# Attention with a threshold search: the test for points in reach only in the last search update, and other places for the work beside a turn

## The chip, the cores and the metric

The kernel runs on one core of one Trainium2 chip. The metric is the device time in microseconds of one execution. Times before the change: 4861.07, 4864.83 and 4874.88 us, median 4864.83. One further execution was taken with the hardware profiler on; the profile and the trace are of that one.

## The reference, cut to what matters

The program is two layers of a network on a tensor of 4 images, 256 channels, 32 x 32 points: attention, a mixture of experts, a selective scan, and a second mixture of experts. The change touches the attention alone. For each image and each of 8 heads it forms 1024 x 1024 scores, keeps in each row the `dyn_k` largest ones (one number for all rows, from the data), takes the softmax over them, and multiplies with the values. A depthwise 3 x 3 convolution of the values is added before the projection:

```python
attn = jnp.einsum('bhdn,bhdm->bhnm', q, k) * SCALE
dyn_k = jnp.floor(N * jnp.mean(g)).astype(jnp.int32)
order = jnp.argsort(-attn, axis=-1)
ranks = jnp.argsort(order, axis=-1)
attn = jnp.where(ranks < dyn_k, attn, -jnp.inf)
attn = jax.nn.softmax(attn, axis=-1)
out = jnp.einsum('bhdn,bhmn->bhdm', v, attn).reshape(Bx, C, Hh, Ww)
pe = lax.conv_general_dilated(v_img, pe_w, ..., feature_group_count=C) + pe_b[None, :, None, None]
return conv1x1(out + pe, proj_w, proj_b)
```

## The kernel before

**Halves and turns.** The scores are cut into 64 halves, in the order image, group of four heads, pair, half: 128 query rows by 1024 keys for four heads. Instead of sorting, the kernel searches for each row the threshold that leaves `dyn_k` scores above it. A half passes through four turns of the pipeline; `turn(i)` (L716) works on half i (h0), i-1 (h1), i-2 (h2) and i-3 (h3) and on one pair of finished halves. 16 turns belong to one image. The order of all instructions is written out by hand (`manual_schedule`, L781): each engine executes its own part of the list in that order.

In a turn, in order: PE forms the second half of h0's scores (`scores(1)`, L526) and ACT copies them out of PSUM (`take`, L534, four copies); PE forms the weights of the pair (`weights`, L637, and L642, which subtracts a large number from the scores that the masks mark: the drop matmuls); DVE takes windows of h3 (L551, L554); DVE makes the first update of the search (`update`, L592, called at L735); ACT counts h0 at the guess (L500, four counts). Then **place 0**. ACT takes the exponential (`exps`, L650), PE multiplies with the values (`sums`, L660); DVE finishes h3's windows; ACT and DVE count h1 (L500, L504). **Place 1.** PE forms the pair's second weights; DVE enters h0 into the search and makes the second update (L759); ACT and DVE count h2; POOL makes the four masks of h3 (`mask`, L584), which wait for the second update by a dependency put in by hand (L585 to L589), and six small operations (`verify`, L573 to L578). **Place 2.** Exponentials, counts of h0. **Place 3.** `start(i + 1)` (L710): first `due` (L706), then the first half of the next scores. Counts of h1, the second `sums`. **Place 4.** The mask buffers are one deep for the odd half of a pair and two deep for the even one (L583).

**The update.** `update` keeps for each row a bracket of two thresholds with their counts. The point just counted replaces one end of it, and a new point is interpolated (L601 to L611). Then L613, L615 and L616 move the point only where the count was not within reach of the aim (plus or minus 7.5): points in reach stay. After the last update the point is kept (L544), counted once more, and the exact threshold is picked among seven scores next to it. If a row's point should not be in reach then, `attention_by_bits` (L787) computes the whole attention again, under an `If` on the data (L966).

**The work beside.** Each place calls `beside(i)` (L691). It takes one stretch from a list `todo` of generators, each with a turn from which it may run and a turn by which it must be done. A generator yields True where a PE stretch has just been issued (its result lies in the only bank "m" of PSUM, L262 of the printed lines' neighbourhood: `bank`), and False after the eviction of that bank; `beside` goes on until a True. So at each place the stretch before is evicted and the next one issued. The generators:

- `Group.steps`: q and k of four heads (L343; evictions L347, L350 on ACT), the transpose of k (L358, eviction L360), second moments (L364; L367 on DVE), mq (L375; L377), mo_ps (L381, L382), then the first guess of the thresholds: L386 to L390 on DVE, a square root as a power on POOL (L391), L394, and in the next step L400 to L405 on DVE. 12 stretches.
- `Image.values`: v transposed (L424, eviction L428 on ACT), 4 stretches.
- `Image.rest`: v padded (L440, L443), for each half of the channels nine diagonals on POOL (L450, one buffer) and the convolution in six stretches of three matmuls (L455, eviction L460 on ACT), then the projection (L468, eviction L472 on DVE). 20 stretches.
- `Image.finish`: the projection of the attention's output (L481, L484), 4 stretches.

Before a turn starts, `due` runs whatever has to be done by then, without a pause. In the kernel before, from turn 16b of image b: group 1 from turn +5 (by +8), values 1 from +8, the rest from +9 (by +20), the next image's group 0 from +13 (by +16), its values 0 from +16, finish from +21 (by +23).

Of the kernel before, what the change touches and what calls it, by code (L numbers as in the profile page):

```python
# [17 lines left out]
ALU = mybir.AluOpType  # L18
# [34 lines left out]
def metaformer(ctx: ExitStack, tc: tile.TileContext, t: dict, out: bass.AP):  # L53
    nc = tc.nc
# [8 lines left out]
    first = cons.tile([P, E], F32, tag="first", name="first")  # L63
# [117 lines left out]
    with ExitStack() as st:  # L181
# [39 lines left out]
        with tc.tile_pool(name="a_ln", bufs=2) as lp, \  # L221
                tc.tile_pool(name="a_lnp", bufs=4, space=PSUM) as psl:
            g1 = load(lp, "g1", [P, CT, P], t["g1"].rearrange("(c p) o -> p c o", p=P))
            for b in range(B):
# [3 lines left out]
                for h in range(NHALF):  # L228
# [9 lines left out]
                    i = b * NHALF + h  # L238
# [350 lines left out]
                                                               mybir.DependencyReason.DATA))  # L589
                    self.drops.append(dr)  # L590

        def update():  # L592

            def flat(a):
                return a.rearrange("p k n j -> p k (n j)")

            st_ = flat(state)
            br = bracket.rearrange("p e k n j -> p e k (n j)")
            t, u = st_[:, 0], st_[:, 1]
            pick = p2.tile([P, 2, R], I32, tag="pick", name="pick", bufs=1)  # L600
            nc.vector.scalar_tensor_tensor(pick, u.unsqueeze(1).to_broadcast([P, 2, R]), aim, side,  # L601
                                           ALU.is_lt, ALU.not_equal)
            nc.vector.copy_predicated(br, pick.unsqueeze(2).to_broadcast([P, 2, 2, R]),
                                      st_.unsqueeze(1).to_broadcast([P, 2, 2, R]))
            dd = p2.tile([P, 2, R], F32, tag="dd", name="dd", bufs=1)
            nc.vector.tensor_tensor(dd, br[:, 1], br[:, 0], ALU.subtract)
            nc.vector.reciprocal(dd[:, 1, :], dd[:, 1, :])
            fr = p2.tile([P, R], F32, tag="fr", name="fr", bufs=1)
            nc.vector.scalar_tensor_tensor(fr, br[:, 0, 1, :], aim, dd[:, 1, :], ALU.subtract, ALU.mult)
            nc.vector.tensor_tensor(fr, fr, dd[:, 0, :], ALU.mult)  # L610
            nc.vector.tensor_tensor(fr, br[:, 0, 0, :], fr, ALU.subtract)  # L611
            low = p2.tile([P, R], F32, tag="low", name="low", bufs=1)
            nc.vector.tensor_scalar(low, u, aim_lo, None, ALU.is_le)  # L613
            move = p2.tile([P, R], I32, tag="move", name="move", bufs=1)
            nc.vector.scalar_tensor_tensor(move, u, aim_hi, low, ALU.is_ge, ALU.add)  # L615
            return nc.vector.copy_predicated(t, move, fr)  # L616

        def to_u(lanes, first_dve):

            ud = state[:, 1, lanes, first_dve:]  # L620
            nc.vector.tensor_scalar(ud, ud, 2.0, -float(L), ALU.mult, ALU.add)
# [52 lines left out]
        groups = {(b, g): Group(b, g) for b in range(B) for g in range(2)}  # L674
        images = [Image(b) for b in range(B)]
# [1 line left out]
        PER = 2 * NT  # L677


        todo = [[0, 0, groups[0, 0].steps(), False], [0, 0, images[0].values(0), False]]  # L680
        for b in range(B):
            i = b * PER
            todo.append([i + 5, i + 8, groups[b, 1].steps(), False])
            todo.append([i + 8, i + 13, images[b].values(1), False])
            if b + 1 < B:
                todo.append([i + 13, i + 16, groups[b + 1, 0].steps(), False])
                todo.append([i + 16, i + 21, images[b + 1].values(0), False])
            todo.append([i + 9, i + 20, images[b].rest(), False])
            todo.append([i + 21, i + 23, images[b].finish(), False])

        def beside(i):  # L691

            while True:
                ready = [w for w in todo if w[0] <= i]
                if not ready:
                    return
                w = next((w for w in ready if w[3]), None) or min(ready, key=lambda w: w[1])
                try:
                    w[3] = next(w[2])
                except StopIteration:  # L700
                    todo.remove(w)
                    w[3] = False
                if w[3]:
                    return

        def due(i):  # L706
            while any(w[1] <= i for w in todo):
                beside(i)

        def start(i):  # L710
            due(i)
            halves.append(Half(i, *order[i]))
            halves[i].group = groups[halves[i].b, halves[i].g]
            halves[i].scores(0)

        def turn(i):  # L716
            def half(d):
                return halves[i - d] if 0 <= i - d < len(halves) else None

            h0, h1, h2, h3 = (half(d) for d in range(4))  # L720

            pair, q = pairs.get((i - 5) // 2 if i % 2 else (i - 6) // 2), 0 if i % 2 else 2
            done = pairs.get((i - 7) // 2) if i % 2 else None

            if h0:
                h0.scores(1)
                h0.take()
            if pair:
                pair.weights(q)
            if h3:  # L730
                h3.window(0)
                h3.window(1)
            if half(1) or half(2):
                to_u(slice(0, 2), FIRST_DVE[1])
                update()  # L735
            if h2:
                h2.keep_threshold()
            if done:
                done.norm()
            if h0:  # L740
                h0.count(4, h0.at_guess)
            beside(i)
# [9 lines left out]
            beside(i)  # L752
            if pair:
                pair.weights(q + 1)
            if h0:
                h0.enter()
            if h1:
                to_u(slice(h1.lane, h1.lane + 1), FIRST_DVE[0])
            after = update() if h0 or h1 else None  # L759
            if h2:  # L760
                h2.count(FIRST_DVE[0], h2.at_last)
            if h3:
                h3.mask(after)
                h3.verify()
                if h3.n == 1:
                    pairs[h3.i // 2] = Pair(halves[h3.i - 1 : h3.i + 1], images[h3.b])
            beside(i)
# [4 lines left out]
            beside(i)  # L772
# [6 lines left out]
            beside(i)  # L779
# [316 lines left out]
    with ExitStack() as st:  # L1096
# [207 lines left out]
        scans, steps, ys, cum = [], iter(()), [], None  # L1304
# [37 lines left out]
        with tc.manual_schedule():  # L1342
            for k in range(-2, len(order) + 1):
                turn(k)
# [5 lines left out]
    with ExitStack() as st:  # L1350
# [12 lines left out]
        with ExitStack() as sa:  # L1363
# [3 lines left out]
            def tmp(name, shape, dt=F32):  # L1367
                return pa.tile([P, *shape], dt, tag=name, name=name)
# [54 lines left out]
            steps = tmp("steps", [NTA * P // T])  # L1423
# [11 lines left out]
            place = tmp("place", [E, NTA])  # L1435
# [175 lines left out]
```

## Time and profile before

| | |
|---|---|
| median of 3 runs | 4864.83 us |
| the profiled execution | 4900.55 us |
| its span, first to last instruction | 4898.8 us |
| mean granted TensorE clock | 0.856 |
| first and last masks of the attention (L584) | 213.0 and 2061.2 us |
| masks, L584 | x256, 724.6 us busy on POOL, 2848 ns each |
| counts on ACT, L500, state | x448, 514.1 us, 1148 ns each |
| counts on DVE, L504, state | x320, 408.6 us, 1277 ns each |
| copies on ACT, L534 | x256, 246.4 us, 1014 ns each |

Of the page, part 1 gives busy time and share for each engine, and part 2 cuts the span into 40 slices of 122 us with the busy share in tenths; the attention lies in slices 2 to 17. Part 5 lists groups of equal instructions with busy time, mean and the idle time before them. A line of the timeline gives start and length in microseconds, engine, line of the kernel, operation, tiles, and in square brackets how long the engine had been idle and what released it.

### The profile page before, as it was taken

To read this page: it belongs to the slowest core of one execution; us is meant where nothing else is said; L and a number is where in the kernel's file an instruction comes from. 1 tells how busy PE (TensorE), PEld (TensorE's weight loads), DVE (VectorE), ACT (ScalarE), POOL (GpSimd) and SP (SyncE) were. 2 spreads that over 40 slices of the span, in tenths; PEclk is the share of its full clock that TensorE was granted. 3 is DMA by queue.
4 is the path that set the end of the run, shared out by engine and by line. 5 is a ranking of instruction groups with operands and counts; after the bars stand their busy time and mean duration, and the time that the engine had idled before them with its cause. 6 is when DMAs were issued, how large, how long until landed. Compare 5 with 4: busy or idle time off the path is not lost.

```text
span 4898.8 us, 51450 instructions
## 1 busy us (share of the span) xinstructions
PE 4004.6 (82%) x18714; PEld 2228.5 (45%) x18714; DVE 3255.5 (66%) x5263; ACT 2894.4 (59%) x3813; POOL 1405.0 (29%) x1126
## 2 busy tenths in 40 slices
PE   7378777877787777689999799989989994599993
PEld 4143434343434343356666333434433432488882
DVE  2687897789778887732223799999999995111212
ACT  3788898788878978522111666677666762122221
POOL 0244444545445454510000122222222223200004
PEclk8578767877797678778999899999999997799995
DMA  3000000000000000010000223323323334334433
GB/s 128 0 1 9 1 1 1 9 1 1 1 9 1 1 1 9 1 36 1 0 1 3 78 92 112 103 87 112 104 86 112 112 111 146 118 115 121 119 109 107
DMA packets 128616, 264.86 MB, mean 54 GB/s; under 512 B 29017, under 2 KB 77282, under 8 KB 127586
## 3 DMA queue, kind: packets, MB, share of 16 engines
q1 hardware_dynamic: 118144, 243.15, 15.3%
q0 software_dynamic: 6144, 16.79, 1.1%
q8 instruction: 150, 2.46, 0.2%
q10 hardware_dynamic: 4066, 1.55, 0.1%
q14 instruction: 112, 0.92, 0.1%
HBM read 224.74 MB, written 36.70 MB: 53 GB/s over the span
## 4 chain that ended last, share of the span: by engine, by line
PE 29%; DVE 19%; issue 3%; SPq 2%; ACT 2%; DMA 1%; POOL 0%; another core or an unknown queue 0%; ACTq 0%; DVEq 0%; POOLq 0%
PE hp L1505 6%; PE yp L1511 6%; PE y L1012 5%; PE hp L1005 5%; DVE h L1284 4%; DVE h L1269 4%; DVE h L1260 4%; PE hp L1255 3%; DVE yc L1294 2%; SPq L1478 2%; DVE h L1278 1%; PE y L1295 1%; PE hp L1288 1%; ACT da_c L1242 0%; PE y L173 0%
## 5 line engine op out<-in xcount | busy, mean ns | idle before, releaser
L584 POOL TENSOR_SCALAR dr<-s_n,last 128x1024 bf16<-128x1024 f32 x256 | 724.6, 2848 | 955.2 <-DVE state L616 598.7
L1240 POOL TENSOR_TENSOR uu<-dx,bb 128x1024 f32<-128x1024 f32 x128 | 317.4, 2480 | 1521.3 <-issue 807.9
L500 ACT ACTIVATE junk_a<-s_n,state 128x1024 int8<-128x1024 f32 x448 | 514.1, 1148 | 21.7 <-DVE state L616 11.7
L1255 PE MATMUL hp<-h,ident 128*128 128x512 f32 x1024 | 496.9, 608 | 27.3 <-DVE h L1278 19.0
L1242 ACT ACTIVATE da_c<-delta,a_log 128x1024 f32<-128x1024 f32 x128 | 270.0, 2109 | 307.1 <-DVE h L1284 307.1
L504 DVE TENSOR_SCALAR_CACHE_REDUCE junk_v<-s_n,state 128x1024 int8<-128x1024 f32 x320 | 408.6, 1277 | 8.0
L1507 ACT ACTIVATE hid<-hp,b 128x256 f32<-128x256 f32 x312 | 145.1, 473 | 415.4 <-PE hp L1505 415.4
L534 ACT COPY s_n<-sp 128x1024 f32<-128x1024 f32 x256 | 246.4, 1014 | 227.0 <-PE sp L526 166.8
L551 DVE SCALAR_TENSOR_TENSOR w<-s_n,win 128x1024 f32<-128x1024 f32 x256 | 359.3, 1403 | 5.5
L1014 DVE SCALAR_TENSOR_TENSOR acc<-y,tk_comb,acc 128x256 f32<-128x256 f32 x256 | 121.0, 484 | 356.0 <-PE y L1012 352.1
L660 PE MATMUL o_ps<-ex,vT 128*32 128x256 f32 x2048 | 274.1, 490 | 83.8 <-ACT ex L650 81.0
L1514 DVE TENSOR_TENSOR ys<-yp,b2e 128x512 f32<-128x512 f32 x39 | 27.0, 692 | 467.4 <-PE yp L1511 467.4
L1255 PEld LDWEIGHTS hp<-h,ident 128*128 128x128 f32 x1024 | 191.3, 193 | 304.3 <-issue 202.5
L554 DVE MAX8 win<-w 128x8 f32<-128x1024 f32 x256 | 314.5, 1228 | 8.8
L1255 PE MATMUL hp<-h,twice 128*128 128x512 f32 x512 | 258.8, 625 | 64.1 <-DVE h L1260 40.6
L500 ACT ACTIVATE junk_a<-s_n,guess 128x1024 int8<-128x1024 f32 x256 | 295.0, 1152 | 6.2
L1260 DVE TENSOR_TENSOR_SCAN h<-da,uu 128x1024 f32<-128x1024 f32 x128 | 290.1, 2266 | 3.6 <-ACT da L1248 3.6
L1284 DVE TENSOR_TENSOR_SCAN h<-da_c,uu 128x1024 f32<-128x1024 f32 x128 | 292.3, 2284 | 0.0
L1007 ACT ACTIVATE hid<-hp,b 128x512 f32<-128x512 f32 x128 | 88.0, 687 | 345.6 <-PE hp L1005 344.8
L1269 DVE TENSOR_TENSOR_SCAN h<-da,uu 128x1024 f32<-128x1024 f32 x128 | 289.9, 2264 | 0.0
L1505 PE MATMUL hp<-xe,w 128*128 128x256 f32 x1248 | 280.8, 383 | 7.5 <-DVE xe L1498 7.5
L650 ACT ACTIVATE ex<-sT 128x1024 f32<-128x1024 f32 x256 | 246.4, 1012 | 63.1 <-PE sT L642 62.7
(480 smaller groups left out, 8147.7 us busy)
## 6 DMA issues: line engine op xcount, KB each, us to landing
bb<-bc_d SPq DMA_DIRECT2D x128, 512.0 KB, 4.8
cb<-bc_d SPq DMA_DIRECT2D x128, 512.0 KB, 4.0
w<-in_w SPq DMA_DIRECT2D x47, 1024.0 KB, 5.0
slots_x<-zeros SPq DMA_DIRECT2D x1, 9984.0 KB, 32.4
xs<-slots_x SPq DMA_DIRECT2D x39, 256.0 KB, 3.1
slots_y<-ys SPq DMA_DIRECT2D x39, 256.0 KB, 2.4
b2e<-in_b SPq DMA_DIRECT2D x39, 128.0 KB, 3.8
x_in<-in_x SPq DMA_DIRECT2D x4, 1024.0 KB, 7.9
```

The lines of the kernel that those rows point to most:

```text
L500: nc.scalar.activation(junk, self.row(r), AF.Sign, bias=thr, scale=-1.0, accum_out=u)
L504: nc.vector.tensor_scalar(junk, self.row(r), thr, None, ALU.is_lt, ALU.add, accum_out=u)
L551: nc.vector.scalar_tensor_tensor(w, self.row(r), self.win[:, r, 0:1], self.row(r), ALU.is_gt if r < LAST_DVE else ALU.is_ge, ALU.subtract, ...
L554: nc.vector.max(out=self.win[:, r, 1:], in_=w)
L584: ins = nc.gpsimd.tensor_scalar(dr, self.row(r), self.last[:, r : r + 1], None, ALU.is_lt)
L1240: nc.gpsimd.tensor_tensor(self.uu[:, 0], self.prep.dx[:, c], self.bb, ALU.mult)
L1255: nc.tensor.matmul(self.hp[h], ident if eye is None else eye, view[:, ts(h, HW // NHALF), :], start=first, stop=False)
L1260: nc.vector.tensor_tensor_scan(rows.rearrange("p r w -> p (r w)"), self.da, self.uu[:, 0], 0.0, ALU.mult, ALU.add)
L1269: nc.vector.tensor_tensor_scan(hs[:, ::-1], self.da[:, ::-1], self.uu[:, 0][:, ::-1], 0.0, ALU.mult, ALU.add)
L1284: nc.vector.tensor_tensor_scan(hs, self.da_c, self.uu[:, 1], 0.0, ALU.mult, ALU.add)
L1505: nc.tensor.matmul(hp[:, f % 2], w1[:, c, ts(f, P)], xe[:, c], start=(c == 0), stop=(c == CT - 1))
L1511: nc.tensor.matmul(yp[:, a], hid[:, f, ts(a, P)], w2e[:, f, :], start=(f == 0), stop=(f == NF - 1))
```

## The change

`update` takes an argument. With `stay=True` (the first update of a turn, which is also the last one of a half) it is as before. With `stay=False` (the second update of a turn) the interpolated point is written to the state at once, and the three instructions of the test are left out. The list of work gets places: a turn is five places, a generator may start at a given place, and takes new stretches only in places that it is given. A stretch that was begun is carried on in any place. `rest` gets places 1 and 3, the groups places 1 to 4, and the groups may start 2 places into the turn that is one earlier than before. `due` has no place: it takes anything that is ready.

```diff
-        def update():
+        def update(stay):
...
             nc.vector.tensor_tensor(fr, fr, dd[:, 0, :], ALU.mult)
+            if not stay:
+                return nc.vector.tensor_tensor(t, br[:, 0, 0, :], fr, ALU.subtract)
             nc.vector.tensor_tensor(fr, br[:, 0, 0, :], fr, ALU.subtract)
...
+        PLACES = 5
+        todo = []
+
+        def plan(first, needed, steps, places=range(PLACES)):
+            todo.append([first, needed, steps, False, places])
+
+        plan(0, 0, groups[0, 0].steps())
+        plan(0, 0, images[0].values(0))
         for b in range(B):
             i = b * PER
-            todo.append([i + 5, i + 8, groups[b, 1].steps(), False])
-            todo.append([i + 8, i + 13, images[b].values(1), False])
+            plan((i + 4) * PLACES + 2, i + 8, groups[b, 1].steps(), (1, 2, 3, 4))
+            plan((i + 8) * PLACES, i + 13, images[b].values(1))
             if b + 1 < B:
-                todo.append([i + 13, i + 16, groups[b + 1, 0].steps(), False])
-                todo.append([i + 16, i + 21, images[b + 1].values(0), False])
-            todo.append([i + 9, i + 20, images[b].rest(), False])
-            todo.append([i + 21, i + 23, images[b].finish(), False])
-
-        def beside(i):
+                plan((i + 12) * PLACES + 2, i + 16, groups[b + 1, 0].steps(), (1, 2, 3, 4))
+                plan((i + 16) * PLACES, i + 21, images[b + 1].values(0))
+            plan((i + 9) * PLACES, i + 20, images[b].rest(), (1, 3))
+            plan((i + 21) * PLACES, i + 23, images[b].finish())
+
+        def beside(i, place=None):
 
             while True:
-                ready = [w for w in todo if w[0] <= i]
-                if not ready:
+                ready = [w for w in todo if w[0] <= i * PLACES + (place or 0) and (place is None or place in w[4])]
+                w = next((w for w in todo if w[3]), None) or min(ready, key=lambda w: w[1], default=None)
+                if w is None:
                     return
-                w = next((w for w in ready if w[3]), None) or min(ready, key=lambda w: w[1])
                 try:
                     w[3] = next(w[2])
                 except StopIteration:
...
                 to_u(slice(0, 2), FIRST_DVE[1])
-                update()
+                update(stay=True)
...
-            after = update() if h0 or h1 else None
+            after = update(stay=False) if h0 or h1 else None
```

The five calls `beside(i)` of a turn become `beside(i, 0)` to `beside(i, 4)`.

More of the change, by code (lines that the diff above doesn't have):

```diff
@@ L677, in metaformer @@
         PER = 2 * NT
-        todo = [[0, 0, groups[0, 0].steps(), False], [0, 0, images[0].values(0), False]]
+        PLACES = 5
[4 more added lines that the diff above has]
+        plan(0, 0, images[0].values(0))
         for b in range(B):
             i = b * PER
-            todo.append([i + 5, i + 8, groups[b, 1].steps(), False])
-            todo.append([i + 8, i + 13, images[b].values(1), False])
+            plan((i + 4) * PLACES + 2, i + 8, groups[b, 1].steps(), (1, 2, 3, 4))
+            plan((i + 8) * PLACES, i + 13, images[b].values(1))
             if b + 1 < B:
-                todo.append([i + 13, i + 16, groups[b + 1, 0].steps(), False])
-                todo.append([i + 16, i + 21, images[b + 1].values(0), False])
-            todo.append([i + 9, i + 20, images[b].rest(), False])
-            todo.append([i + 21, i + 23, images[b].finish(), False])
-        def beside(i):
+                plan((i + 12) * PLACES + 2, i + 16, groups[b + 1, 0].steps(), (1, 2, 3, 4))
[3 more added lines that the diff above has]
+        def beside(i, place=None):
             while True:
-                ready = [w for w in todo if w[0] <= i]
-                if not ready:
+                ready = [w for w in todo if w[0] <= i * PLACES + (place or 0) and (place is None or place in w[4])]
+                w = next((w for w in todo if w[3]), None) or min(ready, key=lambda w: w[1], default=None)
+                if w is None:
                     return
-                w = next((w for w in ready if w[3]), None) or min(ready, key=lambda w: w[1])
                 try:
@@ L741, in turn @@
                 h0.count(4, h0.at_guess)
-            beside(i)
+            beside(i, 0)
             if pair:
@@ L751, in turn @@
                 h1.count(FIRST_DVE[0], h1.at_state)
-            beside(i)
+            beside(i, 1)
             if pair:
@@ L766, in turn @@
                     pairs[h3.i // 2] = Pair(halves[h3.i - 1 : h3.i + 1], images[h3.b])
-            beside(i)
+            beside(i, 2)
             if pair:
@@ L771, in turn @@
                 h0.count(FIRST_DVE[1], h0.at_state)
-            beside(i)
+            beside(i, 3)
             if i + 1 < len(order):
@@ L778, in turn @@
                 pair.sums(q + 1)
-            beside(i)
+            beside(i, 4)
         with tc.manual_schedule():
```

## The prediction

> **What bounds the kernel now.** I read the page first, then the timeline of each engine in the stage that the diff touches, from about 150 to 2060 us. On the page of the kernel before:
>
> ```profile
> PE 4004.6 (82%) x18714; PEld 2228.5 (45%) x18714; DVE 3255.5 (66%) x5263; ACT 2894.4 (59%) x3813; POOL 1405.0 (29%) x1126
> ...
> PEclk8578767877797678778999899999999997799995
> ```
>
> The shares are averages over four stages; only the first third is attention, and there the share of the span tells little: ACT, DVE and PE are each busy 75 to 85%. So I looked for what ends last in one quiet turn (no stretch beside it), turn 18. POOL, ACT and DVE in the timeline:
>
> ```profile
> 650.14 11.30 POOL L584 TENSOR_SCALAR dr<-s_n,last 128x1024 bf16<-128x1024 f32 x4 [13.24 <-DVE state L616]
> ...
> 676.85 11.30 POOL L584 TENSOR_SCALAR dr<-s_n,last 128x1024 bf16<-128x1024 f32 x4 [13.82 <-DVE state L616]
> ```
> ```profile
> 661.47 1.93 ACT L534 COPY s_n<-sp 128x1024 f32<-128x1024 f32 x2 [1.35 <-POOL dr L584]
> ```
> ```profile
> 647.75 0.23 DVE L601 SCALAR_TENSOR_TENSOR pick<-state,aim,side 128x16 int32<-128x16 f32 x1 [1.75 <-ACT junk_a L500]
> ...
> 649.17 0.17 DVE L611 TENSOR_TENSOR fr<-bracket,fr 128x8 f32<-128x8 f32 x1
> ...
> 649.77 0.17 DVE L616 COPY_PREDICATED state<-move,fr 128x8 f32<-128x8 int32 x1
> ```
>
> This is a ring: masks on POOL (11.3 us), then ACT's last two copies wait for the last mask, four guess counts, two exps, three state counts (12.3 us from 661.47 to 673.8), then the second update on DVE (2.2 us), then 0.2 us to the next masks. One round is 26.1 us when ACT is last and 26.7 when DVE is (turn 19, where the norm of a pair adds 2.2 us to DVE). I measure turns from mask start to mask start (POOL timeline). From turn 20 to turn 36, one image, old: 20 to 24 127.6 us, 24 to 28 129.7, 28 to 31 89.0, 31 to 32 26.1, 32 to 36 105.7; sum 478.1, where 16 quiet turns would take 422. The rest, 56 us an image, is what the stretches beside the turns cost.
>
> **Part 1, the update.** 65 times three instructions (L613, L615, L616) go, and L611 writes the state itself. On the ring that is 649.94 (end of L616) less 649.34 (end of L611): 0.60 us a turn, and quiet turns become 25.5 and 26.1. It pays only where masks wait for DVE. In even turns the masks of the odd half (one buffer) also wait for PE's drop matmuls, whose first quarter ended at 649.1; so 0.4 us of slack to PE are left there. 0.6 times 65, 39 us, is the upper end, nothing the lower.
>
> **Part 2, the stretches move.** Following the new plan by hand and in the changed kernel's instruction order, the same 20 conv stretches, 12 group stretches, 4 of values and 4 of finish run in other places. Prices: a conv stretch of three matmuls took 2.84 us or 4.21 (rows below), one of two 128x512 matmuls 2.0 to 2.75, a vT one 1.9 to 2.1. PE waits 2.88 us at place 0 of a quiet turn, so that place hides a stretch; places 1 and 2 to 4 have 0.4 to 1.6 us.
>
> - Turns 24 to 28: the conv's first eight stretches were five a turn, and now are two or three. One at place 1 of an odd turn is free (its masks have a second buffer); in an even one it costs its length less 0.4. I get 26.3 + 27.8 + 26.1 + 33.0 = 113.2, 16.5 less. The 33.0: a conv stretch at place 1 of turn 27 leaves PE 3 to 4 us late, two more precede the next scores, and one at place 1 of turn 28 precedes its drops.
> - Turns 20 to 24, the group with finish. Starting it a turn earlier puts q and k stretches at places 2, 3, 4 of turn 20, each waiting for ACT's eviction of the one before, as in old turn 29, where ACT's copies ended 3.1 us late. 30.4 + 29.7 + 30.6 + 38.6 = 129.3, 1.7 more. The last is as before: guess is still forced at the end of turn 23 and waits for POOL (row 809.70 below).
> - Turns 28 to 31: conv and group mixed; mp leaves place 1 of an even turn (2 us less): 29.4 + 29.4 + 29.6 = 88.4, 0.6 less.
> - Turns 32 to 36: conv, values and proj in turns that were quiet: 28.6 + 28.2 + 27.6 + 25.6 = 110.0, 4.3 more.
> - Turn 31 to 32 is the step that decides. The group now reaches its square root (L391 on POOL) at place 3, behind the four masks of the turn, not ahead of them. The forced call then evicts the guess and goes on to the next stretch that is ready: the first conv matmuls of the second half of channels, whose nine diagonals (L450) stand behind the square root on POOL. In PE's order these three matmuls come before the next half's scores. The old trace shows both waits apart:
>
> ```profile
> 804.23 5.44 POOL L391 TENSOR_TENSOR sd<-sd,half 128x32 f32<-128x32 f32 x1
> ```
> ```profile
> 809.70 0.25 DVE L400 SCALAR_TENSOR_TENSOR guess<-sd,z,mo 128x32 f32<-128x32 f32 x1 [6.97 <-POOL sd L391]
> ```
> ```profile
> 870.92 6.95 POOL L450 TENSOR_SCALAR diag<-ident,pe_w 128x128 f32<-128x128 f32 x9
> ```
> ```profile
> 871.58 2.84 PE L455 MATMUL ap__6310<-vpad,diag 128*128 128x512 f32 x6 [1.07 <-POOL diag L450]
> ...
> 929.81 4.21 PE L455 MATMUL ap__6771<-vpad,diag 128*128 128x512 f32 x6 [1.92 <-ACT x L460]
> ```
>
> Masks and the six small POOL operations take 12.9 us (791.38 to 804.23), the square root 5.4: the first diagonal is ready 19.0 us after the masks began, the third 20.6. PE would reach this point about 5 us after it, so it idles some 14 us, with the scores behind it: scores 1.1 to 2.1, sums 1.8 to 3.4, the next conv stretch 2.8 to 4.2, half of the next scores 0.6 to 1. ACT's second copy starts at 27.5 to 32 and the copies end at 30.5 to 35, against 13.3 in a quiet turn. Plus 10.5 to the end of the state counts, and then, because a conv stretch at place 1 of even turn 32 waits for ACT's eviction (0.7), runs (2.8 to 4.2) and precedes the drops (1.5 to 2.4): 46 to 53. I take 49.5, 23.4 more. It happens three times (turns 15, 31, 47).
>
> What the Trainium skill says against the change: "TensorE: Matmul & The Clock Gate", Part 1, "What's actually happening", holds that the array's clock is throttled by default and released by sustained activity. The rows 871.58 and 929.81 (2.84 and 4.21 us for the same work) and the PEclk digits of 7 and 8 here, 9 later, agree. By that rule a thinner conv would run its stretches nearer to 4.2, and with all nine exposed stretches of an image at that end the sum would grow by about 6 us an image.
>
> **The sum.** An image in the middle: +1.7 - 16.5 - 0.6 + 23.4 + 4.3 = +12.3, twice. The first image (turns 3 to 20, 490 us): its first group is spread without a finish, -6; conv -14; -0.6; +23.4; +4.2: +7. The last: +1.7 - 14.5, and its second conv half runs on in turns 60 to 64, +9: -4. The update in the first turns: -1. Sum 7 + 24.6 - 4 - 1 = +26 us in the profiled execution (4900.55 us, its span 4898.8). That execution lies 36 us above the median of 4864.83; I carry the difference over: 4891 us.
>
> **Rivals.**
> - The guess alone (no change): if PE does not lose its 14 us, because DVE's late guess holds the turn anyway. The old turn 23 to 24, with that wait, took 39.2; less 0.6 gives 38.6 for 31 to 32, 11 less than mine, three times: 26 - 33 = -7, 4858 us. For it: the same DVE wait of 6.97 us is there. Against: ACT's copies need PE's scores, and PE's queue has the conv matmuls ahead of them.
> - Faster, the other side: the slack of PE takes up what is put at places 2 to 4, so that the update's 0.6 us is paid out in turns 20 to 24, 28 to 31 and 32 to 36 as well. Old times less 0.6 a turn: 4.1 + 1.2 + 6.7 = 12 less an image, three times, and 11 in the last: 26 - 47 = -21, 4844 us. It decides once such stretches delay ACT's second copy by less than about 1.3 us (the wait for POOL at 661.47). Against: old turn 29 lost 3.1 us in this way.
> - The count at the last update misses its window without the test before it, and the whole attention runs again by bits: 4 x 8 x 256 counts of 1.277 us (L504) are 10.5 ms more. The last update keeps the test and its bracket is only narrower; 1 in 100.
>
> **Chances.** Forecast 0.55; worse still 0.03; guess alone 0.22; faster 0.19; by bits 0.01. About 0.3%, 15 us, is what this measurement can tell from no change. Faster 0.19, same 0.22, slower 0.59. The range: three stalls of 38.6 and half of the second rival's gain give 4848, stalls of 53 and half of the conv's gain lost 4925; the gain of the update is between its ends in both.
>
> **What would show it.** Masks 25.5 and 26.1 us apart in quiet turns for part 1. In turns 15, 31, 47 a PE wait of 10 us or more for diag L450, and mask to mask of 46 or more: if it is under 40, the decisive step is wrong. Turns 24 to 28 near 113 us. If turns 20 to 24 and 32 to 36 come out below the old 127.6 and 105.7, the second rival holds.

## The result and the profile after

The changed kernel takes 4884.84 us (median of 4 runs, 4880.53 to 4887.95) against 4865.09 us before (median of 4, 4861.07 to 4874.88): a ratio of 1.0037, 95% interval 1.0019 to 1.0055. It is slower by 20 us. Run once more with the experiments, on another chip, it took 4911.9 against 4890.25 us: 1.0044 (1.0027 to 1.0061). The chips differ by 25 to 31 us for one and the same kernel before, so from here on times are compared as ratios and differences within one chip; spans inside the attention are compared over chips, and each is of a single profiled execution. The profiled executions are no total either: what follows the last masks is untouched by the change and took 2837.6 us in the profile of before (4898.8 less 2061.2), 2809.1 in the first profile of the changed kernel (4878.8 less 2069.7) and 2826.0 in the second.

The page of the changed kernel, first profile:

```profile
PE 3963.8 (81%) x18714; PEld 2195.7 (45%) x18714; DVE 3211.0 (66%) x5068; ACT 2897.6 (59%) x3813; POOL 1416.6 (29%) x1126
...
PEclk8577777777777777888999899999999997799996
```

195 DVE instructions less (65 times three), a little less of PE and DVE, the same clock of 0.856: nothing here tells that the kernel is slower. So first a turn that shows the ring alone: turn 60, in which PE has conv stretches to run, but nothing waits for them. POOL, ACT and DVE:

```profile
1920.28 11.30 POOL L584 TENSOR_SCALAR dr<-s_n,last 128x1024 bf16<-128x1024 f32 x4 [16.70 <-DVE junk_v L504]
...
1945.76 2.85 POOL L584 TENSOR_SCALAR dr<-s_n,last 128x1024 bf16<-128x1024 f32 x1 [5.57 <-DVE state L612]
```
```profile
1931.61 1.93 ACT L534 COPY s_n<-sp 128x1024 f32<-128x1024 f32 x2 [0.57 <-POOL dr L584]
```
```profile
1944.02 0.23 DVE L601 SCALAR_TENSOR_TENSOR pick<-state,aim,side 128x16 int32<-128x16 f32 x1 [1.86 <-ACT junk_a L500]
...
1945.43 0.17 DVE L612 TENSOR_TENSOR state<-bracket,fr 128x8 f32<-128x8 f32 x1
```

The ring is the same, and it is 25.48 us long, not 26.1: the second update ends with L612 at 1945.60, 1.58 us after its first instruction, where it took 2.2. Part 1 does what it says.

Now turn 31. POOL, DVE and PE:

```profile
1035.87 11.30 POOL L584 TENSOR_SCALAR dr<-s_n,last 128x1024 bf16<-128x1024 f32 x4 [13.95 <-DVE state L612]
...
1048.71 5.44 POOL L391 TENSOR_TENSOR sd<-sd,half 128x32 f32<-128x32 f32 x1
1054.14 6.04 POOL L450 TENSOR_SCALAR diag<-ident,pe_w 128x128 f32<-128x128 f32 x9
1084.81 2.85 POOL L584 TENSOR_SCALAR dr<-s_n,last 128x1024 bf16<-128x1024 f32 x1 [24.62 <-PE sT L644]
```
```profile
1054.19 0.36 DVE L400 SCALAR_TENSOR_TENSOR guess<-sd,z,mo 128x32 f32<-128x32 f32 x1 [12.60 <-POOL sd L391]
```
```profile
1054.81 4.86 PE L455 MATMUL ap__7583<-vpad,diag 128*128 128x512 f32 x6 [14.42 <-POOL diag L450]
1059.60 1.14 PE L526 MATMUL sp<-k__6858,q 16*128 16x512 f32 x8
...
1065.31 1.14 PE L526 MATMUL sp<-k__6858,q 16*128 16x512 f32 x8
...
1080.40 2.84 PE L455 MATMUL ap__7737<-vpad,diag 128*128 128x512 f32 x6 [2.32 <-ACT x L460]
```
```profile
1060.83 1.01 ACT L534 COPY s_n<-sp 128x1024 f32<-128x1024 f32 x1 [17.50 <-PE sp L526]
1066.48 2.84 ACT L534 COPY s_n<-sp 128x1024 f32<-128x1024 f32 x3 [4.64 <-PE sp L526]
```

Read it from POOL: four masks, six small operations, the square root, the diagonals, without a gap from 1035.87 to 1060.2. DVE waits 12.6 us for the square root, PE 14.4 us for the first diagonal; the scores (L526) are behind PE's wait, and ACT's copies behind the scores. The next masks come 48.94 us after the last ones, where it was 26.13. The operand of the square root was there at 1041.6 (DVE, L390), 7.1 us before POOL began it. In the kernel before, turn 31 has the square root ahead of its masks, and no diagonals behind them:

```profile
1043.83 5.46 POOL L391 TENSOR_TENSOR sd<-sd,half 128x32 f32<-128x32 f32 x1 [12.02 <-DVE sd L390]
1049.28 11.30 POOL L584 TENSOR_SCALAR dr<-s_n,last 128x1024 bf16<-128x1024 f32 x4
```

The Trainium skill says as much ("PSUM — Partial Sum Buffer", "Engine vs sequencer instructions": the queues of ScalarE, VectorE and GpSimd, here ACT, DVE and POOL, are strictly first in, first out, and matmuls start in program order).

One view adds this up over the whole execution. What ended the idle time ahead of the instructions on the tile diag (us, times), in the changed kernel, and in the kernel before:

```profile
  POOL diag L450: 85.9, 12
```
```profile
  POOL diag L450: 6.7, 12
```

All stages, in us from mask start to mask start (L584), with the numbers of the prediction. The second column of the changed kernel is its second profile:

| turns | before | predicted | changed | changed, again |
|---|---|---|---|---|
| 3 to 20 | 490.0 | 497 | 499.6 | 499.4 |
| 20 to 24 | 127.6 | 129.3 | 133.5 | 133.1 |
| 24 to 28 | 129.7 | 113.2 | 109.2 | 109.2 |
| 28 to 31 | 89.0 | 88.4 | 85.0 | 90.0 |
| 31 to 32 | 26.1 | 49.5 | 48.9 | 51.4 |
| 32 to 36 | 105.7 | 110.0 | 108.5 | 107.8 |
| 20 to 36, one image | 478.1 | 490.4 | 485.1 | 491.5 |
| 52 to 65, the last | 380.4 | 376 | 370.6 | 370.1 |
| 3 to 65 | 1826.8 | | 1839.6 | 1852.6 |

The conv spread over more turns gives 20 us an image, and the turn of the guess takes 23 to 25 of them back.

### The profile page after: what moved, and what is told of

It is laid out like the page before. It is cut to its first block, busy times and chain, and to the rows that moved or that the text cites. A ratio compares the mean times of both kernels' runs of the same rounds, so it can differ in the third digit from the quotient of the medians.

```text
span 4878.8 us, 51245 instructions
## 1 busy us (share of the span) xinstructions
PE 3963.8 (81%) x18714; PEld 2195.7 (45%) x18714; DVE 3211.0 (66%) x5068; ACT 2897.6 (59%) x3813; POOL 1416.6 (29%) x1126
## 5 line engine op out<-in xcount | busy, mean ns | idle before, releaser
L584 POOL TENSOR_SCALAR dr<-s_n,last 128x1024 bf16<-128x1024 f32 x256 | 729.8, 2868 | 995.1 <-DVE state L612 501.3
L500 ACT ACTIVATE junk_a<-s_n,state 128x1024 int8<-128x1024 f32 x448 | 514.3, 1148 | 25.9 <-DVE state L618 12.1
L1265 PE MATMUL hp<-h,ident 128*128 128x512 f32 x1024 | 499.6, 611 | 27.1 <-DVE h L1288 18.9
L662 PE MATMUL o_ps<-ex,vT 128*32 128x256 f32 x2048 | 305.3, 514 | 182.7 <-ACT ex L652 177.4
L551 DVE SCALAR_TENSOR_TENSOR w<-s_n,win 128x1024 f32<-128x1024 f32 x256 | 349.1, 1364 | 5.4
L662 PE MATMUL o_ps<-ex,ones 128*32 128x256 f32 x2048 | 290.6, 502 | 0.0
## 6 DMA issues: line engine op xcount, KB each, us to landing
slots_x<-zeros SPq DMA_DIRECT2D x1, 9984.0 KB, 31.9
```

Of the source, the lines that this page charges most:

```text
L500: nc.scalar.activation(junk, self.row(r), AF.Sign, bias=thr, scale=-1.0, accum_out=u)
L551: nc.vector.scalar_tensor_tensor(w, self.row(r), self.win[:, r, 0:1], self.row(r), ALU.is_gt if r < LAST_DVE else ALU.is_ge, ALU.subtract, ...
L584: ins = nc.gpsimd.tensor_scalar(dr, self.row(r), self.last[:, r : r + 1], None, ALU.is_lt)
L662: nc.tensor.matmul(self.o_ps[32 * j : 32 * j + 32, w], ones if w else vT[:, m, ts(j, HD)], self.ex[j // 2][:, j % 2, mm], start=(m == 0 an ...
L1265: nc.tensor.matmul(self.hp[h], ident if eye is None else eye, view[:, ts(h, HW // NHALF), :], start=first, stop=False)
```

## The experiments

Eleven more runs followed, one of them the changed kernel itself. Two theories were to be told apart first. Mine: POOL's order makes the long turn, in two steps; the square root behind the masks makes the guess late, and the diagonals behind both hold PE with the next scores behind it. The rival: the late guess alone holds the turn.

| run | against before, us (ratio, 95%) | 20 to 24 | 24 to 28 | 28 to 31 | 31 to 32 | 3 to 65 |
|---|---|---|---|---|---|---|
| update_only | -22.9 (0.9946 to 0.9973) | 128.8 | 126.7 | 91.9 | 26.2 | 1811.1 |
| places_only | +37.9 (1.0071 to 1.0098) | 137.5 | 111.0 | 87.3 | 49.6 | 1865.7 |
| due_needed | -8.9 (0.9976 to 0.9995) | 136.0 | 109.2 | 86.8 | 38.6 | 1829.5 |
| diag_act | -17.4 (0.9955 to 0.9980) | 136.5 | 109.1 | 90.0 | 39.8 | 1819.9 |
| after_again | +21.7 (1.0027 to 1.0061) | 133.1 | 109.2 | 90.0 | 51.4 | 1852.6 |
| group_all | -38.2 (0.9900 to 0.9933) | 131.2 | 110.8 | 89.1 | 28.4 | 1791.2 |
| conv_only | -20.6 (one run) | 125.8 | 109.8 | 88.7 | 46.2 | 1805.3 |
| groups_only | +31.9 (one run) | 136.6 | 129.1 | 96.2 | 25.8 | 1864.8 |
| diag_soon | -12.9 (0.9967 to 0.9988) | 134.6 | 109.2 | 90.1 | 39.9 | 1819.9 |
| best1 | -68.8 (0.9847 to 0.9879) | 124.3 | 108.9 | 91.7 | 28.8 | 1760.7 |
| best2 | -83.6 (0.9820 to 0.9853) | 125.3 | 110.2 | 86.0 | 28.4 | 1740.0 |

**The two parts alone.** update_only is the kernel before with part 1 of the change, and places_only the changed kernel with the old second update:

```diff
-        def update():
+        def update(stay):
...
+            if not stay:
+                return nc.vector.tensor_tensor(t, br[:, 0, 0, :], fr, ALU.subtract)
...
-                update()
+                update(stay=True)
...
-            after = update() if h0 or h1 else None
+            after = update(stay=False) if h0 or h1 else None
```
```diff
-            after = update(stay=False) if h0 or h1 else None
+            after = update(stay=True) if h0 or h1 else None
```

> The kernel before with the shorter second update alone; all stretches stay in their old places. Ring theory: each turn whose masks wait for DVE gets 0.6 us shorter, quiet turns 25.5 and 26.1 us as in the changed kernel; with 65 turns the total falls by 20 us (10 to 39). Rival, that the turns which have a stretch beside them are set by PE or ACT and take the gain up: only the 15 or so quiet turns gain, under 10 us in all. Either way turns 31 to 32 stay at 25.5 to 26.1 us.

> The changed kernel with the old second update (test, bracket half and copy kept): the moved stretches alone. If the two parts add up, it is slower than the changed kernel by what the update alone gains over the kernel before, 10 to 39 us, so 30 to 59 us over the kernel before; quiet turns 26.1 and 26.7 us again, turn 31 to 32 at 48.9 to 50. Rival, that the moved stretches pay and the update costs: within 6 us of the kernel before or under it.

Both fell as expected: the update gains 22.9 us, the places lose 37.9. Together that is a loss of 15 us, and 20 to 22 were measured for both parts at once. after_again is the changed kernel itself, beside the later runs:

> The changed kernel once more, on the chip of the other experiments. Its first profiled execution shows attention ending 8.5 us later than in the kernel before (masks of turn 65), while the medians on another chip stood 19.8 us apart. If the trace tells the whole: 5 to 13 us over the kernel before. If something after attention also loses: 16 to 24 us over it.

It is 21.7 us over the kernel before, and its attention ends 25.3 us later (last masks 2086.5 against 2061.2): the loss lies in the attention, not behind it, though the total is in the range that was expected for a loss behind it. The 8.5 us that the first profile showed were too few because turns 28 to 32 and 44 to 48 were 7.5 and 7.4 us shorter there, and the first masks began 3.8 us earlier (208.6 against 212.4).

From the two parts alone: quiet turns are 25.5 and 26.1 with the update, 26.1 and 26.6 without. The rivals of both expectations fall. The update is not paid everywhere in these profiles: from 20 to 24 and 28 to 31 update_only is 1.3 and 2.9 us longer than before, from 24 to 28 it gains 3.0, all with the same order of work otherwise; turns with stretches do not repeat that well from one execution to the next (the granted clock has a part in it, see the end of the next section).

**The long turn, from three sides.** due_needed lets the forced call take due work only:

```diff
-        def beside(i, place=None):
+        def beside(i, place=None, forced=False):
...
-                ready = [w for w in todo if w[0] <= i * PLACES + (place or 0) and (place is None or place in w[4])]
+                ready = [w for w in todo if w[0] <= i * PLACES + (place or 0) and (place is None or place in w[4])
+                         and (not forced or w[1] <= i)]
...
-                beside(i)
+                beside(i, None, True)
```

> The changed kernel, but the call that forces a due piece of work takes only work that is due: at the end of turns 15, 31 and 47 the guess is still forced, and the first three conv matmuls of the second half of channels, whose diagonals stand behind the square root, are not (they come in turns 33 and 34, and the last two proj stretches are forced at the end of turn 35 instead). My theory, that PE's wait for these diagonals makes the stall: turn 31 to 32 falls from 48.9 to 38.6 to 41 us, three times, minus 24 to 31 us, of which up to 10 us come back in turns 33 to 36; total minus 15 to minus 30 us against the changed kernel. Rival, that the late guess alone holds the turn: 31 to 32 stays within 2 us of 48.9 and the total within 8 us of the changed kernel or above.

diag_act has the diagonals of the second half made on ACT:

```diff
+                        if c:
+                            nc.scalar.activation(diag[:, k, :], ident, AF.Identity, scale=pe_w[:, c, k : k + 1])
+                        else:
                             nc.gpsimd.tensor_scalar(diag[:, k, :], ident, pe_w[:, c, k : k + 1], None, ALU.mult)
```

> The changed kernel with the nine diagonals of the second half of channels made on ACT, not on POOL; the order of PE is the same, and the guess is forced as before. My theory (PE waits for POOL's diagonals, and the scores stand behind): PE's wait in turns 15, 31 and 47 goes, turn 31 to 32 falls to 39 to 43 us (ACT has nine small copies more ahead of the scores' copies, an estimated 2 to 3 us), total minus 18 to minus 30 us against the changed kernel. Rival, that the guess alone holds the turn: 31 to 32 stays at 48 to 52, total the same or up to 9 us more.

diag_soon issues them on POOL in turn 28, behind the last conv matmul of the first half:

```diff
-                for c in range(CT):
+                def diagonals(c):
                     diag = wk.tile([P, 9, P], F32, tag="diag", name="diag")
...
+                    return diag
+
+                diag = diagonals(0)
+                for c in range(CT):
...
                         nc.scalar.activation(x[b][:, c, ts(h, HALF)], ap_, AF.Identity, bias=pe_b[:, c : c + 1])
+                        if c + 1 < CT and h + 1 == NHALF:
+                            diag = diagonals(c + 1)
                         yield False
```

> The changed kernel, but POOL makes the diagonals of the second half of channels right after the last conv matmul of the first half (turn 28), three turns before they are used. The guess is still forced at the end of turns 15, 31, 47. My theory: the first conv matmuls there run at once, and only the late guess is left: turn 31 to 32 is 38.6 us as in the run where the due call took only due work, not 49 to 51; minus 25 to 38 us against the changed kernel in all. Rival, that these matmuls hold PE for another reason (clock, bank): 44 us or more.

Turn 31 to 32 falls to 38.6, 39.8 and 39.9 us, and the totals lie 31, 39 and 35 us below the changed kernel's +21.7. The turn is where it was expected each time; of the totals, that of due_needed is at the end of its range (15 to 30 us), and that of diag_act 9 us beyond it (18 to 30). Turn 31 in the timelines: PE of diag_soon, PE of diag_act, and ACT of diag_act with the nine diagonals (the added lines shift the numbers; L458 and L459 are L455):

```profile
1035.45 4.81 PE L459 MATMUL ap__7583<-vpad,diag 128*128 128x512 f32 x6 [0.32 <-DVE mo L386]
```
```profile
1041.40 4.70 PE L458 MATMUL ap__7583<-vpad,diag 128*128 128x512 f32 x6 [0.55 <-ACT diag L451]
```
```profile
1040.97 2.72 ACT L451 ACTIVATE diag<-ident,pe_w 128x128 f32<-128x128 f32 x9
```

The wait of 14.42 is now 0.32 and 0.55, with the same matmuls in the same place of PE's order. What is left is the guess; POOL and DVE of due_needed:

```profile
1032.93 11.30 POOL L584 TENSOR_SCALAR dr<-s_n,last 128x1024 bf16<-128x1024 f32 x4 [16.85 <-ACT junk_a L500]
...
1045.77 5.44 POOL L391 TENSOR_TENSOR sd<-sd,half 128x32 f32<-128x32 f32 x1
```
```profile
1051.25 0.25 DVE L400 SCALAR_TENSOR_TENSOR guess<-sd,z,mo 128x32 f32<-128x32 f32 x1 [9.79 <-POOL sd L391]
```

So the guess makes 12 to 14 us of the 23 to 25, and the diagonals the other 9 to 13: both steps are in it, and the rival is half of the truth. In due_needed a part of the gain comes back: 32 to 36, where the end of the projection is now forced, is 2.7 us longer than in the changed kernel's first profile. 20 to 24 is 2.5 us longer too, but there the clock of PE was lower (see the next section).

**Which part of the places costs.** conv_only has the groups where they were, groups_only has the conv in all five places:

```diff
-            plan((i + 4) * PLACES + 2, i + 8, groups[b, 1].steps(), (1, 2, 3, 4))
+            plan((i + 5) * PLACES, i + 8, groups[b, 1].steps())
...
-                plan((i + 12) * PLACES + 2, i + 16, groups[b + 1, 0].steps(), (1, 2, 3, 4))
+                plan((i + 13) * PLACES, i + 16, groups[b + 1, 0].steps())
```
```diff
-            plan((i + 9) * PLACES, i + 20, images[b].rest(), (1, 3))
+            plan((i + 9) * PLACES, i + 20, images[b].rest())
```

> The short update and the convolution in two places, but the groups where they were before (start at turns 5 and 13 of each 16, all places). In turn 31 the guess is done at place 2 and nothing is forced; the first three conv matmuls of the second half of channels come at place 3, ahead of the next scores, and their diagonals stand behind the masks, though not behind the square root. My theory (diagonals behind POOL's masks hold PE): turn 31 to 32 is the changed kernel's 48.9 less the square root's 5.4, 41 to 45 us, without any forced call. Rival, that a forced late guess is what makes the long turn: 26 to 29 us. Turns 24 to 28 stay at 109 us, 20 to 24 go back to 126 to 129, 28 to 31 to 88 to 92.

> The short update and the groups as in the change (earlier, places 1 to 4), but the convolution in all five places as before. In turn 31 the square root comes at place 0, the guess at place 1, and no diagonals are left to make. My theory: 31 to 32 is 26 to 28 us; 20 to 24 stays at 133 to 137 (the earlier q and k stretches cost 5 us there, whatever the conv does), 24 to 28 goes back to 126 to 129, 28 to 31 is 88 to 92. If 20 to 24 goes back to 127 to 129 instead, the loss there came from the conv.

In conv_only the guess is there when the masks begin, nothing is forced, and turn 31 to 32 still takes 46.2 us (43.0 in turn 47), where 41 to 45 were expected. POOL, then PE:

```profile
1017.32 5.46 POOL L391 TENSOR_TENSOR sd<-sd,half 128x32 f32<-128x32 f32 x1 [9.94 <-DVE sd L390]
1022.77 11.30 POOL L584 TENSOR_SCALAR dr<-s_n,last 128x1024 bf16<-128x1024 f32 x4
1035.67 6.83 POOL L450 TENSOR_SCALAR diag<-ident,pe_w 128x128 f32<-128x128 f32 x9
```
```profile
1036.33 5.49 PE L455 MATMUL ap__7583<-vpad,diag 128*128 128x512 f32 x6 [15.90 <-POOL diag L450]
```

Here the diagonals alone do it. The two waits do not add: each alone makes the turn 39 to 46, both 49 to 51. groups_only shows the other cost that I had put too low: 20 to 24 takes 136.6 us, as expected, and 28 to 31 takes 96.2, where 88 to 92 were expected. Turn 20 of it, PE and ACT:

```profile
713.15 3.78 PE L343 MATMUL qp<-x,wqk 128*128 128x512 f32 x4 [4.61 <-ACT q L347]
716.86 2.09 PE L526 MATMUL sp<-k__3017,q 16*128 16x512 f32 x8
```
```profile
712.43 0.67 ACT L347 ACTIVATE q<-qp,bqk 128x512 f32<-128x512 f32 x1
...
725.33 2.84 ACT L534 COPY s_n<-sp 128x1024 f32<-128x1024 f32 x3 [5.27 <-PE sp L526]
```

The second q stretch waits until ACT, busy with counts, evicts the first one from the only bank; the scores are behind it, and ACT's copies wait for them. Turn 20 to 21 takes 34.8 us, and 26.7 in conv_only, which starts its group with turn 21. (The changed kernel, with the same plan for its groups, takes 31.5; the other 3.3 us go with a lower clock, see the next section.) Against update_only, which differs by the groups alone, groups_only is 54 us longer from 3 to 65; conv_only is 6 us shorter, though it pays three long turns of 43 to 46.

**Groups in all places.** group_all only opens place 0 to the groups of the changed kernel, in both of their lines:

```diff
-            plan((i + 4) * PLACES + 2, i + 8, groups[b, 1].steps(), (1, 2, 3, 4))
+            plan((i + 4) * PLACES + 2, i + 8, groups[b, 1].steps())
```

> The changed kernel with the group's stretches allowed in all five places, place 0 too; start as in the change. The group then comes to its square root at place 0 of turns 15, 31, 47, ahead of the turn's masks on POOL, the guess at place 1, and nothing is forced there; in turns 7, 23, 39, 55 the square root comes at place 2, the guess at place 3, and nothing is forced either. My theory (each of these turns pays for a square root and for diagonals standing behind the masks): turn 31 to 32 falls from 48.9 to 27 to 31 us (diagonals ahead of the masks too, as the conv stretch follows at place 1), 23 to 24 from 38.6 to 27 to 33 us; minus 18 to 22 three times and minus 6 to 11 four times, up to 20 us back elsewhere: minus 60 to minus 100 us against the changed kernel. Rival, that the conv spread over the turns itself or PE's load makes the long turn: 31 to 32 stays over 38 us, total within 25 us of the changed kernel.

31 to 32 falls to 28.4 as expected, and the total lies 60 us below the changed kernel, the least of what was expected. But 23 to 24 stays at 38.58, which I had expected at 27 to 33, though nothing is forced there any more. POOL and DVE in turn 23:

```profile
795.96 11.31 POOL L584 TENSOR_SCALAR dr<-s_n,last 128x1024 bf16<-128x1024 f32 x4 [14.12 <-DVE state L612]
808.82 5.45 POOL L391 TENSOR_TENSOR sd<-sd,half 128x32 f32<-128x32 f32 x1
```
```profile
814.30 0.25 DVE L400 SCALAR_TENSOR_TENSOR guess<-sd,z,mo 128x32 f32<-128x32 f32 x1 [13.91 <-POOL sd L391]
```

The square root at place 2 is issued behind the masks of the turn, and that alone sets the length: guess 18.3 us after the masks began, first update (L601, behind two counts and two windows on DVE) at 27.1, state counts on ACT from 29.4, next masks at 38.58. Turn 23 to 24 took 38.5 to 38.6 in every run that has the new update and the square root behind the masks, forced or not.

**A version that beats both.** best1 is conv_only with the early diagonals of diag_soon. best2 also starts the second group at place 2 of turn 20 (from the second image on) and makes its mo_ps stretches one, so that the square root is issued at place 1 of turn 23:

```diff
-                    if n % 4 == 3:
+                    if n == NT - 1:
...
-            plan((i + 5) * PLACES, i + 8, groups[b, 1].steps())
+            plan((i + 4) * PLACES + 2 if b else 5 * PLACES, i + 8, groups[b, 1].steps())
```

> Short update, convolution in two places, groups where they were before, and the diagonals of the second half made in turn 28. Nothing stands behind the masks in turn 31 any more. My theory: 31 to 32 falls from 43 to 46 us to 26 to 28.5, three times; total 50 us (45 to 60) under the run with the conv moved alone, 65 to 80 us under the kernel before. Rival, that the first conv matmuls at place 3 of turn 31 hold the next scores anyway: 31 to 32 stays over 33.

> As the last one, but from the second image on the second group starts at place 2 of its turn 4 (all places open to it) and its eight mean-and-spread matmul pairs are one stretch, so that the square root is issued at place 1 of turn 23, ahead of the masks, and the guess is not late. My theory: 23 to 24 falls from 38.6 to 26 to 30 us, while 20 to 21 rises from 26.7 to 31 to 35 and 22 to 23 stays under 30: 20 to 24 falls by 0 to 8 us, three times; 0 to 25 us less in all than the run before it. If the square root at place 1 still delays the masks or the guess, 23 to 24 stays at 38.6 and it is up to 25 us slower.

best1: 31 to 32 takes 28.75 us in all three images, a little over the 28.5 I had expected, and the total is 48 us under conv_only's one run (each against the kernel before on its chip). Against diag_soon, which differs by the plan of the groups alone, it is 56 us faster: so much do the moved groups cost, 11 us of it in turn 31 to 32 and 9 in 20 to 24 of each image. best2, turn 23, POOL and DVE:

```profile
772.86 5.46 POOL L391 TENSOR_TENSOR sd<-sd,half 128x32 f32<-128x32 f32 x1 [15.75 <-DVE sd L390]
778.32 11.31 POOL L590 TENSOR_SCALAR dr<-s_n,last 128x1024 bf16<-128x1024 f32 x4
```
```profile
778.36 1.11 DVE L400 SCALAR_TENSOR_TENSOR guess<-sd,z,mo 128x32 f32<-128x32 f32 x1 [2.40 <-POOL sd L391]
```

The square root is ahead of the masks, and 23 to 24 falls from 38.6 to 25.5 to 25.9. The early q and k stretches take most of it back: 20 to 21 is 34.8, 31.1 and 34.8 us in the three images, against 26.3 to 26.7, and 22 to 23 is 31.8 to 34.5, where I had expected less than 30. From 20 to 24 only the third image gains (118.9 against 125.8). More of its 15 us comes from the one stretch of mo_ps elsewhere (30 to 31 and its like in the other images 26.4, against 28.8 to 29.1). The two edits of best2 were not run apart. best2 is 1.6% faster than the kernel before.

## Why the prediction was right, step by step

The side, the mechanism and the time were right: 4891 forecast, 4884.84 measured on the chip of the medians, +26 forecast, +20 and +22 measured. That the sum came so close is in part luck: single terms are off by 2 to 6 us on both sides and cancel. The image from 20 to 36 was forecast at +12.3; it took +6.9 in the first profile and +13.4 in the second.

- **Part 1.** Right: 25.5 and 26.1 in the quiet turns of update_only, 22.9 us in all, between the ends of 0 and 39.
- **Turn 31 to 32, the step that decides.** Right in each part: first diagonal 19.0 us forecast, PE's first matmul 18.9 after the masks began; PE idle 14, measured 14.42 (12.17 in the second profile); ACT's second copy at 27.5 to 32, measured 30.6; copies' end at 30.5 to 35, measured 33.5; turn 49.5, measured 48.9 and 51.4. due_needed, diag_act, diag_soon and conv_only show that both waits are needed for it.
- **Turns 24 to 28.** The mechanism was right, the gain too small: 16.5 forecast, 20.5 measured. The step is the 33.0 of turn 27, which took 29.6: the stretch at place 1 and two more cost less than each one's length.
- **The clock.** In the kernel before, the same stretch took 2.84 us in one place and 4.21 in another, and I had kept up to 6 us an image for a thinner conv. It did not come: all matmuls of L455 together are busy 144.4 us in the attention, 155.0 before. From 24 to 28 the granted clock did fall (0.85 before, 0.74 after), but not under the conv: its matmuls there have a median of 592 ns, as before, and none is over 0.70 us, where some took 1.06 to 1.19. Slow is the first stretch of turn 31: 4.86 us, at a clock of 0.57, and the next one 2.85, at 1.00. The wait of 14.42 us ahead of it is not needed for that, though: in diag_soon the same stretch took 4.81 us behind 0.32 us of idle time. By the Trainium skill ("TensorE: Matmul & The Clock Gate", "What's actually happening") the gate closes after an idle window of about 3.4 us and opens after as long a busy one. With the busy time of the profile that does not come out here: in the changed kernel the clock fell from 1.00 to 0.50 at 1035.0 us, where PE had been busy all of the 3.3 us before and was busy 5.39 of the 5.40 us behind, up to 1040.4, when its wait began. In diag_soon it was 0.50 from 1020.0 to 1035.45, while PE was busy 15.13 of these 15.45 us, almost half of them with matmuls of four columns. What the gate counts as busy, no run here shows.
- **Turns 20 to 24 and 3 to 20.** Too low: +1.7 forecast, +5.9 and +5.5 measured; +7 against +9.6. The step is "30.4 + 29.7 + 30.6 + 38.6": turn 20 to 21 took 31.5 and turn 22 to 23 32.9. I had the mechanism of the q and k stretches waiting for ACT's eviction, but sized it by the 3.1 us of old turn 29, and took the transposes and the next stretches of turn 22 as nearly free. groups_only gives 34.8 and 33.0 for these two; the step from 31.5 to 34.8 goes with a lower clock (below).
- **Turns 28 to 31 and 32 to 36.** 28 to 31: -0.6 forecast, -4.0 in the first profile and +1.0 in the second, with the same program. 32 to 36: +4.3 forecast, +2.8 and +2.1 measured.
- **The last image.** -4 forecast, -9.8 measured: the second half of the conv in turns 60 to 64 cost 2.9 us, not the 9 that I added; turns 60 and 62 hide theirs whole (25.5 us). Turns 56 to 60 gain 18.5, not 14.5.
- **The rivals.** The guess alone gives 38.6, as priced, and is half of the turn's loss. Of the faster rival, turns 20 to 24 and 32 to 36 stay above the old 127.6 and 105.7, so it falls. The repeat by bits did not come. (The upper end of the range, 4925, halves the conv's gain of three images; with that of the fourth it would be 4932.)

The same program took 85.0 us from 28 to 31 in one execution and 90.0 in another, and 2.5 more from 31 to 32. The granted clock is where the two part. In turn 29 they run alike, to 0.02 us on PE, for the first 7.6 us after the masks began. Then the clock of the second one falls: over the 10 us from 6 to 16 us after the masks it is 0.66, against 0.99. The first half of the next scores on PE and ACT's last copies, in the first profile and in the second:

```profile
987.67 1.14 PE L526 MATMUL sp<-k__4889,q 16*128 16x512 f32 x8
```
```profile
992.37 2.84 ACT L534 COPY s_n<-sp 128x1024 f32<-128x1024 f32 x3 [2.45 <-PE sp L526]
```
```profile
991.36 2.09 PE L526 MATMUL sp<-k__4889,q 16*128 16x512 f32 x8
```
```profile
998.85 2.84 ACT L534 COPY s_n<-sp 128x1024 f32<-128x1024 f32 x3 [4.30 <-PE sp L526]
```

Turn 29's masks began at 978.21 and 981.46, so the copies come 14.2 and 17.4 us after them, and turn 29 to 30 takes 30.8 and 33.0 us. Turn 20 to 21 goes the same way, and so do 36 to 37 and 52 to 53. In the runs that start the group in that turn, it took 31.1 to 31.5 us where the clock from 6 to 16 us was 0.83 to 0.86, 32.3 to 32.7 at 0.77 or 0.78, and 33.6 to 35.0 at 0.50 to 0.56. So 2 to 4 us of a turn with stretches can go with the clock, with the same work in the same order. It does not vary at random alone: the changed kernel has the higher one in all three images, groups_only the lower one in all three. What makes it fall, and when, is not settled.

## What to carry to other kernels

When work is moved within a hand-made order, follow every instruction that it issues onto its engine's queue and ask what stands ahead of it there at the new time, small helper work on the slow engine first: the diagonals cost 5 to 7 us of POOL in any place, and 9 to 17 us of everyone's time in one. Operands that depend on constants only could be made turns ahead here for nothing; a result that the next stage waits for has to be issued ahead of the long job on its engine, and whether it is forced or comes in its turn does not matter. A gain measured in one stage (20 us an image) is checked against the stage where the same work comes back. And before a few microseconds of one turn are put down to an edit, read the granted clock of that turn in both profiles.

## What the runs showed of the hardware

Nine 128x128 copies with a scale took 2.72 us on ACT and 5.3 to 7.1 us on POOL; the run that moved half of them to ACT came out 39 us below the changed kernel. A turn set by the masks and the square root repeats to 0.06 us in all runs with the new update and the square root behind the masks (23 to 24, 39 to 40 and 55 to 56: 38.55 to 38.61), while the three turns from 28 to 31 differ by 5 us between two executions of one program. The stages behind the attention, the same in all these kernels, took between 2809 and 2838 us in the three profiled executions of the kernel before and the changed one.
